# Sum of squares from a Gram matrix on TensorE, in a Fourier-layer tokenizer followed by a transformer layer

## The chip, the cores and the metric

The kernel runs on one core of one Trainium2 chip. The metric is the device time of one execution in microseconds. All data is float32. The engines are named as in the profile: PE is TensorE (PEld its weight loads), DVE is VectorE, ACT is ScalarE, POOL is GpSimd, SP is the engine whose queue issues most of the DMA.

## The reference, cut to what matters

64 images of 256x256 are lifted to 32 channels and pass four Fourier layers. Each layer adds a product in the frequency domain (12 frequencies along each edge) to a pointwise 32x32 product over the channels, normalises each channel by the mean and variance over all images and pixels, and applies a ReLU (not in the last). The resulting rows, with 77 text rows, go through one attention and one feed-forward block, which the change doesn't touch.

```python
for i in range(L):
    x1 = _fourier_layer(v, W1, W2)
    x2 = jnp.einsum('bcxy,cd->bdxy', v, w_w[i]) + w_b[i][None, :, None, None]
    v = x1 + x2
    mean = jnp.mean(v, axis=(0, 2, 3), keepdims=True)
    var = jnp.var(v, axis=(0, 2, 3), keepdims=True)
    v = (v - mean) * jax.lax.rsqrt(var + BN_EPS)
    v = v * bn_g[i][None, :, None, None] + bn_b[i][None, :, None, None]
    if i < L - 1:
        v = jax.nn.relu(v)
```

For the variance of layer i+1 the kernel needs, for each channel d, the sum over all pixels of the square of (v W)[d], where W is the pointwise matrix of layer i+1. The rest of the variance comes from the few frequencies.

## The kernel before

The kernel alternates two kinds of stage. `mix(i, ...)` multiplies the frequencies by the weights and works out the scale and shift of the normalisation. `layer(i, ...)` (three times, i = 0, 1, 2) then makes the image of the layer, applies the ReLU, stores it to memory, and takes the next layer's frequencies from it. After the last mix comes the transformer stage.

Inside `layer` the order of instructions is written out by hand: a loop over the images b, and in it over eight tiles t of an image, issues the steps below, and each engine runs its instructions in that order. One tile is 128 partitions (four row bands n of 32 channels) by 2048 pixels.

- `spread(b)` (L595 on PE, L599 on DVE): the inverse transform along x of image b, two PSUM tiles, each transposed by DVE into `y_`. It is issued at t=5 of the image before.
- `pre(b, t)`: the inverse transform along y (L614) and, in layers 1 and 2, the pointwise product of the layer's input `vin` (L625), accumulated in two PSUM tiles of two banks. ACT evicts the first with a ReLU (L632), DVE the second (L633), into the SBUF tile `vo`. SP stores `vo` (L634), and DVE transposes it in 32x32 blocks into `t32` (L637), one `t32` for two tiles; so `t32` holds pixels on partitions and channels along the free axis.
- `product(b, t)`, issued one tile behind `pre`: the next layer's pointwise product of `vo` (L649, 16 matmuls of 32x32 by 512) into two more PSUM tiles; ACT squares each and sums it along the row into a column of `acc` (L656).
- `along_y(b - 1)` at t=1: the forward transform along y of the four `t32` of the image before (L666, 128 matmuls), two PSUM tiles, transposed by DVE into `zt` (L676).
- `along_x(b - 1)` at t=3: the forward transform along x (L689), copied by ACT (L696) and stored (L697).

The loads of `vin` are issued on SP four tiles ahead. All PSUM tiles of a layer come from one ring `lp` of four tiles of two banks, the whole of the PSUM, used in turn: an instruction that writes a tile waits for the readers of the tile that had the place before.

After a layer, `squares(i, acc)` sums `acc` along the row, and a matmul with the table `CHAN` adds the partitions of the same channel, which gives `u2` to `mix`.

Of the kernel before, what the change touches and what calls it, by code (L numbers as in the profile page):

```python
# [9 lines left out]
F32 = mybir.dt.float32  # L10
# [24 lines left out]
def _tables():  # L35
# [47 lines left out]
    out["chan"] = p[:, None] % C == np.arange(C)[None, :]  # L83
# [46 lines left out]
def tile_fno_fusion_transformer(ctx: ExitStack, tc: tile.TileContext, a, cst_d, grid_d, out):  # L130
# [17 lines left out]
    tab = tables(const, "fyt", "chan", "cst")  # L148
# [3 lines left out]
    T4, ID, ONES, CHAN = tab("t4"), tab("ident"), tab("ones"), tab("chan")  # L152
# [336 lines left out]
    def squares(i, acc):  # L489

        u2 = const.tile([128, C], F32, name=f"u2_{i}")
        with tc.tile_pool(name="sq", bufs=1) as sp, tc.tile_pool(name="sqp", bufs=1, space=PSUM) as pp:
            r = sp.tile([128, 1], F32, name="r")
            nc.vector.reduce_sum(r, acc, axis=AX.X)
            rb = sp.tile([128, 128], F32, name="rb")
            nc.vector.tensor_copy(rb, r.to_broadcast([128, 128]))
            ps = pp.tile([128, C], F32, name="ps")
            nc.tensor.matmul(ps, lhsT=rb, rhs=CHAN, start=True, stop=True)
            nc.vector.tensor_copy(u2, ps)
        return u2  # L500

    def layer(i, st, src, dst, acc):
# [7 lines left out]
        with ExitStack() as cx:  # L510
# [9 lines left out]
            pp = pool("lp", 4, space=PSUM)  # L520
# [38 lines left out]
            am, y_, t32, vin, vo = {}, {}, {}, {}, {}  # L559
# [49 lines left out]
            def pre(b, t):  # L609
# [20 lines left out]
                o = vo[b, t] = op.tile([128, 8, S], F32, name="vo")  # L630
                of = o.rearrange("p (n r) y -> p n (r y)", r=2)
                nc.scalar.activation(of[:, 0:2], t2[0], AF.Relu)  # L632
                nc.vector.tensor_scalar(of[:, 2:4], t2[1], 0.0, None, ALU.max)  # L633
# [8 lines left out]
            def product(b, t):  # L642

                o = vo.pop((b, t))
                t2, ps = four()
                for k in range(4):
                    for n in range(4):
                        j = (n + k) % 4
                        nc.tensor.matmul(  # L649
                            ps[n][32 * j:32 * j + 32], lhsT=w4[i + 1][32 * n:32 * n + 32],  # L650
                            rhs=o[32 * n:32 * n + 32, 2 * j:2 * j + 2, :], start=True, stop=True,
                            skip_group_check=True, tile_position=(32 * n, 32 * j),
                        )
                for n in range(2):
                    at = 2 * (8 * b + t) + n
                    nc.scalar.activation(t2[n], t2[n], AF.Square, accum_out=acc[:, at:at + 1])  # L656
# [3 lines left out]
            def along_y(b):  # L660
# [11 lines left out]
                for j in range(4):  # L672
                    t32.pop((b, j))
                zt = zts[b] = zp.tile([128, 2, 32, C], F32, name="zt")
                for h in range(2):
                    nc.vector.transpose(  # L676
                        zt[:, h].rearrange("p k c -> p c k"),
                        t2[h].rearrange("p n (s c) -> p c (n s)", c=C),
                    )

            def along_x(b):
                zt = zts.pop(b)
                ps = pp.tile([128, 2, 512], F32, name="ring")
                for g in range(3):
                    n = 0
                    for h in range(2):
                        for r in range(2):
                            k0 = M * r + 4 * g
                            nc.tensor.matmul(  # L689
                                ps[:, 0, 96 * g:96 * g + 96],  # L690
# [5 lines left out]
                nc.scalar.copy(xo, ps[:, 0, 0:288].rearrange("p (g k) -> p g k", g=3)[:, :, 0:2 * KX])  # L696
# [10 lines left out]
            for b in range(B + 1):  # L707
                for t in range(8):
# [5 lines left out]
                    pb, pt = (b, t - 1) if t else (b - 1, 7)  # L714
                    if pb >= 0 and (b < B or t == 0):
                        product(pb, pt)
                    if b and t == 1:
                        along_y(b - 1)
                    if b and t == 3:
                        along_x(b - 1)  # L720
# [11 lines left out]
    acc = None  # L732
    for i in range(L):
        with tc.tile_pool(name="wn", bufs=2 if i else 1, reuse_waits="tile") as wnp, \
# [7 lines left out]
            else:  # L742
# [4 lines left out]
                u2 = squares(i, acc)  # L747
# [4 lines left out]
        if i < L - 1:  # L752
            acc = const.tile([128, 16 * B], F32, name="acc") if acc is None else acc
            with tc.manual_schedule():
                layer(i, st, vd[(i + 1) % 2], vd[i % 2], acc)
# [374 lines left out]
```

## Time and profile before

| what | us |
|---|---|
| median of three runs | 12480.16 |
| lowest and highest | 12466.59, 12493.44 |
| the profiled execution | 12478.37 |
| its span | 12476.6 |

| stretch (first `along_y` of the layer to the next stage), us | PE | DVE | ACT | PE clock | DMA share | GB/s |
|---|---|---|---|---|---|---|
| 293.8 to 3109.3, layer 0 | 2563.29 | 2177.00 | 1572.51 | 0.94 | 0.53 | 201 |
| 3305.9 to 6405.0, layer 1 | 2863.01 | 2217.49 | 1605.67 | 0.99 | 0.90 | 348 |
| 6603.4 to 9693.9, layer 2 | 2856.29 | 2216.19 | 1605.88 | 0.99 | 0.90 | 349 |
| 9693.9 to 12476.0, end of layer 2, last mix, transformer | 2575.19 | 1807.21 | 1013.60 | 0.97 | 0.58 | 220 |

How to read it: the second table gives busy time of each engine in each stretch. Matmuls are pipelined and the recorded ends overlap, so a busy PE isn't PE at its peak. The DMA share is the mean over the core's 16 DMA engines. In the profile's rows, "128*64 128x512" means a stationary operand of 128 rows and 64 columns and a moving one of 128 rows and 512 columns; an arrow after a stretch of idle time names what ended it, and "issue" means that the profile shows nothing that the engine waited for.

### The profile page before, as it was taken

The numbers are of one execution on the slowest core, as the hardware profiler recorded it, in microseconds if no ns is written. First come the engines' busy times: TensorE is split into PE (matmuls) and PEld (weight loads), VectorE is DVE, ScalarE is ACT, GpSimd is POOL, SyncE is SP. The second block draws the span as 40 slices with busy tenths as digits, with TensorE's granted clock in tenths as the row PEclk, the third lists the DMA queues.
The fourth block names the chain that finished last, engine by engine and source line by source line (L and its number), as shares of the span: only waits on it lengthen the run. The fifth ranks groups of instructions, "written<-read, shape, count | busy, mean of one in ns | idle before, by whom it ended". The sixth has DMA issues, their size and how long they took to land. (4 is left out here: it accounts for less than half of the span.)

```text
span 12476.6 us, 405217 instructions
## 1 busy us (share of the span) xinstructions
PE 11172.7 (90%) x182038; PEld 5874.2 (47%) x182038; DVE 8784.2 (70%) x10531; ACT 6065.1 (49%) x10217; POOL 1529.5 (12%) x2040
## 2 busy tenths in 40 slices
PE   4999999999699999999969999999999599999999
PEld 2444444444344444444434444444444366666666
DVE  4777777777677777777767776777777566666665
ACT  4555555555455555555545555555555333333333
POOL 1000000000100000000010000000000233333333
PEclk7999999999799999999989999999999799999999
DMA  6555555555899899889889898899899755555553
GB/s 187 199 202 202 201 202 202 200 201 203 286 350 350 346 351 353 344 345 349 341 277 358 345 354 347 341 351 352 345 352 352 255 218 229 232 227 221 221 231 151
DMA packets 588469, 3485.04 MB, mean 279 GB/s; under 512 B 96616, under 2 KB 146152, under 8 KB 189800
## 3 DMA queue, kind: packets, MB, share of 16 engines
q1 hardware_dynamic: 540288, 3405.18, 70.9%
q0 software_dynamic: 38144, 50.22, 1.8%
q8 instruction: 1423, 23.31, 0.7%
q10 hardware_dynamic: 8296, 3.72, 0.1%
q14 instruction: 318, 2.61, 0.1%
HBM read 1761.83 MB, written 1696.92 MB: 277 GB/s over the span
## 5 line engine op out<-in xcount | busy, mean ns | idle before, releaser
L656 ACT ACTIVATE ring<-ring 128x1024 f32<-128x1024 f32 x3072 | 3108.8, 1012 | 1185.5 <-PE ring L649 1148.6
L637 DVE STREAM_TRANSPOSE t<-vo 128x2048 f32<-128x2048 f32 x1536 | 3550.1, 2311 | 175.2 <-ACT vo L632 13.5
L649 PE MATMUL ring<-vo,w 32*32 32x512 f32 x49152 | 2851.0, 625 | 385.4 <-DVE zt L676 134.1
L632 ACT ACTIVATE vo<-ring 128x1024 f32<-128x1024 f32 x1536 | 1568.1, 1021 | 3045.8 <-PE ring L625 2386.1
L633 DVE TENSOR_SCALAR vo<-ring 128x1024 f32<-128x1024 f32 x1536 | 1858.6, 1210 | 615.0 <-PE ring L625 420.5
L666 PE MATMUL ring<-t,cst 32*32 32x512 f32 x49152 | 1867.6, 603 | 297.8 <-issue 296.6
L676 DVE STREAM_TRANSPOSE zt<-ring 128x1024 f32<-128x1024 f32 x384 | 712.3, 1926 | 1646.6 <-PE ring L666 1646.6
L649 PEld LDWEIGHTS ring<-vo,w 32*32 32x32 f32 x49152 | 765.5, 105 | 1886.4 <-ACT ring L656 473.7
L584 POOL TENSOR_TENSOR ams<-am,sk 48x512 f32<-48x512 f32 x384 | 486.7, 1268 | 8538.7 <-DMA am<-mix 8218.2
L666 PEld LDWEIGHTS ring<-t,cst 32*32 32x32 f32 x49152 | 976.3, 103 | 1145.6 <-issue 688.7
L625 PE MATMUL ring<-vin,ws 32*32 32x512 f32 x32768 | 1241.9, 607 | 21.2 <-issue 19.2
L689 PEld LDWEIGHTS ring<-cst,zt 128*128 128x128 f32 x4608 | 536.1, 194 | 179.4 <-ACT vo L632 159.5
L1079 POOL DMA_DIRECT2D out_dram<-o x1024 | 512.3, 509 | 660.1 <-DVE o L1074 628.8
L656 ACT ACTIVATION_READ_ACCUMULATOR ring<-ring 128x1 f32 x3072 | 584.2, 190 | 0.0
L689 PE MATMUL ring<-cst,zt 128*128 128x96 f32 x4608 | 568.3, 280 | 8.3 <-DVE zt L676 8.3
L878 PE MATMUL hp<-ch,win 128*32 128x512 f32 x4096 | 473.3, 602 | 8.6 <-DMA ch<-v 8.5
L595 PE MATMUL ring<-ams,cst 49*128 49x512 f32 (+1 forms) x1536 | 391.5, 620 | 99.4 <-POOL ams L584 88.7
L625 PEld LDWEIGHTS ring<-vin,ws 32*32 32x32 f32 x32768 | 253.8, 103 | 410.0 <-issue 382.8
L883 ACT ACTIVATE h<-hp,hbias 128x512 f32<-128x512 f32 x64 | 44.0, 687 | 597.5 <-PE hp L878 581.4
L412 PE MATMUL mps<-wm,xh 32*64 32x128 f32 (+1 forms) x4608 | 110.4, 354 | 242.2 <-DMA xh<-xh 110.8
L595 PEld LDWEIGHTS ring<-ams,cst 49*128 49x128 f32 (+1 forms) x1536 | 147.5, 188 | 349.8 <-issue 242.1
L1041 PE MATMUL pp<-zs,w 128*128 128x165 f32 x2048 | 302.4, 305 | 0.0
(932 smaller groups left out, 12039.4 us busy)
## 6 DMA issues: line engine op xcount, KB each, us to landing
v<-vo SPq DMA_DIRECT2D x1536, 1024.0 KB
vin<-v SPq DMA_DIRECT2D x1024, 1024.0 KB
ch<-v SPq DMA_DIRECT2D x512, 1024.0 KB
mix<-ob SPq DMA_DIRECT2D x192, 256.0 KB
am<-mix SPq DMA_DIRECT2D x384, 96.0 KB
xin<-in_x_dram SPq DMA_DIRECT2D x16, 1024.0 KB
mv<-in_x_dram SPq DMA_DIRECT2D x256, 64.0 KB
out_dram<-o POOLq DMA_DIRECT2D x1024, 16.0 KB, 3.0
```

Of the source, the lines that this page charges most:

```text
L584: nc.gpsimd.tensor_tensor(ams[b % 2][hv], a_[hv], sk[hv].rearrange("p c k -> p (c k)"), ALU.mult)
L595: nc.tensor.matmul(ps[:, n, :], lhsT=EX[hv, 128 * h:128 * h + 128], rhs=ams[b % 2][hv], start=True, stop=True, skip_group_check=True,)
L625: nc.tensor.matmul(ps[n][32 * j:32 * j + 32], lhsT=ws[32 * n:32 * n + 32], rhs=v[32 * n:32 * n + 32, 2 * j:2 * j + 2, :], start=False, sto ...
L632: nc.scalar.activation(of[:, 0:2], t2[0], AF.Relu)
L633: nc.vector.tensor_scalar(of[:, 2:4], t2[1], 0.0, None, ALU.max)
L637: nc.vector.transpose(t32[b, t // 2][:, :, 8 * (t % 2):8 * (t % 2) + 8, :].rearrange("p y s c -> p s y c"), o.rearrange("p s (y l) -> p s ...
L649: nc.tensor.matmul(ps[n][32 * j:32 * j + 32], lhsT=w4[i + 1][32 * n:32 * n + 32], rhs=o[32 * n:32 * n + 32, 2 * j:2 * j + 2, :], start=Tru ...
L656: nc.scalar.activation(t2[n], t2[n], AF.Square, accum_out=acc[:, at:at + 1])
L666: nc.tensor.matmul(ps[n][32 * j:32 * j + 32], lhsT=FYT[32 * n:32 * n + 32, k, :], rhs=t32[b, j][32 * n:32 * n + 32, k].rearrange("p s c -> ...
L676: nc.vector.transpose(zt[:, h].rearrange("p k c -> p c k"), t2[h].rearrange("p n (s c) -> p c (n s)", c=C),)
L689: nc.tensor.matmul(ps[:, 0, 96 * g:96 * g + 96], lhsT=zt[:, h, k0:k0 + 4, :].rearrange("p k c -> p (k c)"), rhs=FX[:, h, 48 * r:48 * r + 9 ...
L1079: nc.gpsimd.dma_start(out[b, 64 * n + 16 * g:64 * n + 16 * g + 16].rearrange("(p t) d -> p t d", t=2), o[32 * g + 8 * n:32 * g + 8 * n + 8 ...
```

## The change

The product of the next layer isn't formed any more. With G the 32x32 Gram matrix of the channels (G[c, c'] is the sum over all pixels of v[c] v[c']), the sum of squares of channel d is the sum over c and c' of W[c, d] G[c, c'] W[c', d].

- `product` and its squares on ACT go. `products(b, j, half)` takes a half of the transposed tile `t32[b, j]`: 32 matmuls, each with the same 128x64 slice as stationary and as moving operand (two pixels of 32 channels), accumulated over the whole image in one 128x64 PSUM tile. Even slices write partitions 0 to 63, odd ones 64 to 127. After the image, DVE adds the tile to `gram` in SBUF. The eight halves of an image are issued at t=3, 4, 5 and 6 (t32 0 and 1), and, an image later, two at t=0 and two at t=1 behind `along_y`.
- Both evictions of `pre` are now made by ACT.
- `along_y` hands its first PSUM tile to ACT, which copies it to `zs`; DVE transposes the second from PSUM and the first from `zs`.
- The ring `lp` has three tiles of two banks; `along_x` and the Gram matrix have one bank each.
- `squares` masks `gram` with a new table `DIAG` (32x32 blocks on the diagonal), multiplies it by W, then by W again element by element, and sums over the partitions with two matmuls.

```diff
@@ -486,20 +486,23 @@
-    def squares(i, acc):
+    def squares(i, gram):
...
-            r = sp.tile([128, 1], F32, name="r")
-            nc.vector.reduce_sum(r, acc, axis=AX.X)
-            rb = sp.tile([128, 128], F32, name="rb")
-            nc.vector.tensor_copy(rb, r.to_broadcast([128, 128]))
+            gm = sp.tile([128, 64], F32, name="gm")
+            nc.vector.tensor_mul(gm, gram, DIAG)
+            ps = pp.tile([128, C], F32, name="gw")
+            nc.tensor.matmul(ps[0:64], lhsT=gm, rhs=w4[i], start=True, stop=True)
+            wgw = sp.tile([64, C], F32, name="wgw")
+            nc.vector.tensor_mul(wgw, ps[0:64], w4[i][0:64])
             ps = pp.tile([128, C], F32, name="ps")
-            nc.tensor.matmul(ps, lhsT=rb, rhs=CHAN, start=True, stop=True)
+            nc.tensor.matmul(ps, lhsT=ONES[0:64], rhs=wgw, start=True, stop=True)
             nc.vector.tensor_copy(u2, ps)
...
-            pp = pool("lp", 4, space=PSUM)
+            pp = pool("lp", 3, space=PSUM)
+            px, pg = pool("lpx", 1, space=PSUM), pool("lpg", 1, space=PSUM)
+            nc.vector.memset(gram, 0.0)
...
-                o = vo[b, t] = op.tile([128, 8, S], F32, name="vo")
+                o = op.tile([128, 8, S], F32, name="vo")
                 of = o.rearrange("p (n r) y -> p n (r y)", r=2)
-                nc.scalar.activation(of[:, 0:2], t2[0], AF.Relu)
-                nc.vector.tensor_scalar(of[:, 2:4], t2[1], 0.0, None, ALU.max)
+                for n in range(2):
+                    nc.scalar.activation(of[:, 2 * n:2 * n + 2], t2[n], AF.Relu)
...
-            def product(b, t):
-
-                o = vo.pop((b, t))
-                t2, ps = four()
-                for k in range(4):
+            def products(b, j, half):
+
+                if (j, half) == (0, 0):
+                    gps[b] = pg.tile([128, 64], F32, name="gp")
+                q = t32[b, j]
+                for y in range(4 * half, 4 * half + 4):
+                    for m in range(8):
+                        d = 64 * (m % 2)
+                        v = q[:, y, 2 * m:2 * m + 2, :].rearrange("p s c -> p (s c)")
+                        nc.tensor.matmul(
+                            gps[b][d:d + 64], lhsT=v, rhs=v, start=(j, y) == (0, 0) and m < 2,
+                            stop=(j, y) == (3, 7) and m > 5, skip_group_check=True,
+                        )
+                if (j, half) == (3, 1):
+                    nc.vector.tensor_add(gram, gram, gps.pop(b))
                     for n in range(4):
-                        j = (n + k) % 4
-                        nc.tensor.matmul(
-                            ps[n][32 * j:32 * j + 32], lhsT=w4[i + 1][32 * n:32 * n + 32],
-                            rhs=o[32 * n:32 * n + 32, 2 * j:2 * j + 2, :], start=True, stop=True,
-                            skip_group_check=True, tile_position=(32 * n, 32 * j),
-                        )
-                for n in range(2):
-                    at = 2 * (8 * b + t) + n
-                    nc.scalar.activation(t2[n], t2[n], AF.Square, accum_out=acc[:, at:at + 1])
+                        t32.pop((b, n))
...
                 zt = zts[b] = zp.tile([128, 2, 32, C], F32, name="zt")
-                for h in range(2):
+                zs = zp.tile([128, 1024], F32, name="zs")
+                nc.scalar.copy(zs, t2[0].rearrange("p n k -> p (n k)"))
+                for h, z in ((1, t2[1].rearrange("p n k -> p (n k)")), (0, zs)):
...
-                ps = pp.tile([128, 2, 512], F32, name="ring")
+                ps = px.tile([128, 288], F32, name="xps")
...
-                    pb, pt = (b, t - 1) if t else (b - 1, 7)
-                    if pb >= 0 and (b < B or t == 0):
-                        product(pb, pt)
-                    if b and t == 1:
-                        along_y(b - 1)
-                    if b and t == 3:
-                        along_x(b - 1)
+                    if b:
+                        if t == 0:
+                            products(b - 1, 2, 0)
+                            products(b - 1, 2, 1)
+                        if t == 1:
+                            along_y(b - 1)
+                            products(b - 1, 3, 0)
+                            products(b - 1, 3, 1)
+                        if t == 3:
+                            along_x(b - 1)
+                    if b < B and t in (3, 4, 5, 6):
+                        products(b, (t - 3) // 2, (t - 3) % 2)
```

## The prediction

> **What bounds the kernel now.** First the page's busy shares and slices, to see which stages there are; then the groups, for the cost of each operation; then the order of time inside one image, because the shares average over stages.
>
> ```profile
> PE 11172.7 (90%) x182038; PEld 5874.2 (47%) x182038; DVE 8784.2 (70%) x10531; ACT 6065.1 (49%) x10217; POOL 1529.5 (12%) x2040
> ...
> PE   4999999999699999999969999999999599999999
> ...
> DMA  6555555555899899889889898899899755555553
> ```
>
> Three long stages of some 9 slices each are the three layer loops of 64 images; the rest (first transform, three mixes, the transformer) is not touched. In the order of time the first `along_y` (L666) of layer 0 starts at 293.8 and the last at 3109.3, 63 images later: 44.7 us an image. Layer 1: 3305.9 to 6405.0, 49.2; layer 2: 6603.4 to 9693.9, 49.1. PE reads as 9 tenths, but its bars overlap and hide waits.
>
> ```profile
> L656 ACT ACTIVATE ring<-ring 128x1024 f32<-128x1024 f32 x3072 | 3108.8, 1012 | 1185.5 <-PE ring L649 1148.6
> L637 DVE STREAM_TRANSPOSE t<-vo 128x2048 f32<-128x2048 f32 x1536 | 3550.1, 2311 | 175.2 <-ACT vo L632 13.5
> L649 PE MATMUL ring<-vo,w 32*32 32x512 f32 x49152 | 2851.0, 625 | 385.4 <-DVE zt L676 134.1
> L632 ACT ACTIVATE vo<-ring 128x1024 f32<-128x1024 f32 x1536 | 1568.1, 1021 | 3045.8 <-PE ring L625 2386.1
> L633 DVE TENSOR_SCALAR vo<-ring 128x1024 f32<-128x1024 f32 x1536 | 1858.6, 1210 | 615.0 <-PE ring L625 420.5
> ```
>
> The columns are total busy time, mean ns, idle time before. L649 shows x49152 = 192 images x 128 matmuls x 2: each float32 matmul is recorded as two passes. One tile step of layer 1 or 2 in order of time (start, length):
>
> ```profile
> 4512.53 0.99 PEld L614 LDWEIGHTS ring<-cst,y__46047 24*128 24x128 f32 x16 [0.91 <-ACT vo L632]
> 4512.53 1.40 PE L614 MATMUL ring<-cst,y__46047 24*128 24x256 f32 x16
> ...
> 4513.86 1.14 PE L625 MATMUL ring<-vin,ws 32*32 32x512 f32 x32
> ...
> 4514.74 1.49 PE L649 MATMUL ring<-vo,w 32*32 32x512 f32 x32
> 4514.74 0.58 PEld L649 LDWEIGHTS ring<-vo,w 32*32 32x32 f32 x31 [0.32 <-issue]
> 4515.15 1.02 ACT L632 ACTIVATE vo<-ring 128x1024 f32<-128x1024 f32 x1 [0.44 <-PE ring L625]
> 4515.21 1.22 DVE L633 TENSOR_SCALAR vo<-ring 128x1024 f32<-128x1024 f32 x1
> ```
>
> The step (3.7 us) is `pre` on PE, then both evictions side by side, then the next `pre`, which waits for its ring slot ("<-ACT vo L632"). The product matmuls L649 run in the shadow of the evictions: they cost PE about 1 us a step (two rounds of 0.43, and a tail) and hardly any time of the image. DVE (1.21 + 2.31 = 3.52 us a step) is nearly as full. Over `along_y` PE is alone: 8.73 us in layer 0 (2000.47 to the next L614 at 2009.20), about 11 in layers 1 and 2, where PE pauses for nothing the profile shows:
>
> ```profile
> 3505.13 6.46 PE L666 MATMUL ring<-t,cst 32*32 32x512 f32 x174
> 3512.84 3.28 PE L666 MATMUL ring<-t,cst 32*32 32x512 f32 x82 [1.25 <-issue]
> 3516.05 1.15 PE L614 MATMUL ring<-cst,y__34227 24*128 24x256 f32 x16
> ```
>
> The DMA table has an instruction queue of 1423 packets and 23.31 MB, 16 KB each. PE has 2 x 182038 matmuls and weight loads: 64 B each, so a packet is 256 of them. I take these pauses for late instruction fetches, since they are long only where DMA is 9 tenths busy. In this image (3505.13 to the next L666 at 3552.99, 47.9) they add to about 3.5 us, so without them layers 1 and 2 stand at 44.4, with a mean of 4.7 us of pauses; layer 0 has images of 43.74 (2000.47 to 2044.21) without any, so 1.0.
>
> **What the Trainium skill says.** "TensorE: Matmul & The Clock Gate", section LDWEIGHTS: a weight load takes its columns / 1.2 ns, whatever the rows. The trace agrees: `along_x` (L689) loads 128 columns 24 times in 2.75 us, (2.75 - 0.19) / 23 = 111 ns against 107. "TensorEngine Tiling (Array Packing)", Key Properties: tiles load and multiply independently, and a change of tiling mode drains the engine. It agrees for the first transform, whose 128x64 tiles are of the new shape: 8 passes of 512 columns took 1.94 us, in four rounds of two, so (1.94 - 0.64) / 3 = 0.43 us a round, 0.85 ns a column, with two at once. But the first page's Part 3 says that loads overlap running matmuls only if the row group differs; in L689 all rows are the same, and a pass of 96 columns (0.08 us) with a load of 111 ns comes every 111 ns: overlapped. I follow the trace.
>
> **The change part by part.**
>
> *Removed, each image:* 8 products on PE, 8 x 1.0 = 8.0 us; 16 squares with accumulator reads on ACT, 16 x (1.01 + 0.19); 8 DVE evictions of 1.21. *Added:* 8 evictions of 1.02 and the copy `zs` (1.0) on ACT. ACT then has 16 x 1.02 + 1.0 + 0.3 = 17.6 us an image; DVE 8 x 2.31 and four transposes of 1.9 = 26. Neither bounds; ACT and DVE gains are worth nothing by themselves.
>
> *Added on PE:* 256 matmuls of a 128x64 stationary and 64 moving columns, on two column tiles in turn: 512 passes, 256 rounds of two. A round is the longer of 64 columns streamed (64 x 0.85 = 54 ns) and 64 loaded (111 / 2 = 56): I take 58, as nothing this short is shown; bounds 54 (both hidden, nothing between) and 112 (load and stream in turn). 256 x 58 = 14.85 us. The six blocks of them (two are double) each pay some 0.25 us of first load and drain: 16.4 us an image. Bounds 13.8 and 30.
>
> *PE's other work:* `pre` from L614 to L625 1.07, L625 with its tail 1.03: 2.1 x 8 = 16.8 (layer 0 without L625: 1.22 x 8 = 9.8); `along_y` 8.7; `along_x` 2.95; `spread` 1.95. With the Gram 46.8 us, layer 0 39.8.
>
> *The ring of three.* A `pre` takes two tiles; the next begins in the third and then needs the first one's eviction. ACT ends that 2.3 us after L625 starts (4513.86 to 4516.17), PE is free after 1.03, and 0.1 of work fits: 1.2 us of wait where no Gram block stands between. That is at t=1 before `along_y`, t=2 and t=7. Elsewhere a block of 2.1 us covers it. At t=5 `spread`'s two tiles follow; `pre` of t=6 needs one back from DVE, which first does the 2.31 transpose behind two serial ACT evictions: 2.4 (ACT) + 2.31 + 1.84 = 6.6 us after the `pre`, PE arrives after 2.12 + 1.95: 2.4 us of wait. Sum 3 x 1.2 + 2.4 = 6.0; bounds 3 and 9. The second eviction moving behind the first makes `vo`, its store on SP, and the `vin` load queued behind that store about 0.9 us later; loads run four tiles ahead, so this is hidden. `zs` lies under 3.9 us of Gram, the two `zt` transposes end 4 us after `along_y`, long before `along_x` at t=3. With own banks for `along_x` and the Gram no further wait is added.
>
> *Pauses.* PE instructions an image go from 1856 to 2368 (layers 1, 2) and from 1344 to 1856 (layer 0). The stretch t=0 and t=1 now has 1216 of them in 22 us. I take 5.0 us of pauses in layers 1 and 2 (DMA has more time per byte, which works against the count), 1.0 in layer 0; bounds 3 and 10.
>
> *Sum.* Layers 1 and 2: 46.8 + 6.0 + 5.0 = 57.8, 8.7 more than 49.1, x128 = 1113. Layer 0: 39.8 + 6.0 + 1.0 = 46.8, 2.1 more than 44.7, x64 = 135. The last image's Gram of each layer stands alone, some 7 us x 3 = 20. `squares` swaps one short chain for another, and the constants grow by 32 columns, read once: nothing. 12476.6 + 1268 = 13745; the runs' median stands 3.6 above the span: 13,750.
>
> **Rivals.** *(A) Instruction supply bounds layers 1 and 2.* If 256 instructions cost 6.1 us there (174 + 82 passes with their loads, 512 instructions, took 10.9, so 5.5 with a stock at hand), 2368 need 56.4 us, and 4 to 5 us of ring waits beside it make 61; layer 0 at 49: 12477 + 1523 + 275 = 14,280. For it: the "issue" pauses; against it: they shrink where DMA has slack. *(B) Loads do not overlap in column tiles.* 112 ns a round, 13.8 us more an image: 12477 + 22.5 x 128 + 15.9 x 64 = 16,370. For it: the skill's sentence; against it L689 and the first transform. *(C) Faster: Gram blocks fill what PE waits for now.* Needed PE work is 46.8 and 39.8, under today's 49.1 and 44.7. If the blocks cover ring waits and fetches run ahead in them, so that these stay under 3.2 us an image together (my sum is 11 and 7), the kernel gains; at 1.5 us it is 12477 - 0.8 x 128 - 3.4 x 64 = 12,160. For it: today's waits end on evictions, which the third tile and the idle DVE relieve. Against it: three places have no block, and pauses grow with instructions.
>
> **How the numbers follow.** Forecast 0.58 (13,300 to 14,000); A 0.18; B 0.08; C 0.10; the remaining 0.06 lies between 12,450 and 13,300, some third of it within 0.2%. A measurement of this kernel can tell about 0.2% from no change. Faster 0.10, same 0.02, slower 0.88. The range from 12,900 to 14,500 takes in A and part of the rest, and leaves out B and C.
>
> **What would show it.** PE as the bound with ACT near 40% and DVE near half in the loops; `along_y` starts 57 to 59 us apart in layers 1 and 2, 46 to 48 in layer 0; a double Gram block (128 passes) of 3.7 to 4 us; PE waits on ACT at t=1, 2 and 7, and on DVE `y_` at t=6. A double block near 7.4 us is B; pauses within Gram blocks over 8 us an image are A; an image under 49 us makes the forecast wrong.

## The result, and the profile after

| | median us | lowest to highest | runs | profiled span |
|---|---|---|---|---|
| before | 12476.82 | 12466.59 to 12493.44 | 4 | 12476.6 |
| after | 13810.66 | 13802.2 to 13825.33 | 4 | 13823.6 |

The ratio is 1.1069 (95% interval 1.105 to 1.1088): the change makes the kernel 10.7% slower. The forecast was 13,750, its range 12,900 to 14,500.

From the page of the changed kernel: busy times, slices, and the queue of the instruction fetches.

```profile
PE 12182.1 (88%) x231196; PEld 8173.4 (59%) x231196; DVE 7036.9 (51%) x9190; ACT 4405.7 (32%) x5801; POOL 1529.6 (11%) x2040
...
PE   5999999996888888888868888888888869999999
...
PEclk7999999997999999999989999999999979999999
DMA  6555555557777777777777777777777775555554
...
q8 instruction: 1807, 29.61, 0.8%
```

DVE fell from 8784 to 7037 us and ACT from 6065 to 4406, and the end moved out by 1347. Layers 1 and 2 fill ten to eleven slices each, and DMA is down from 9 tenths to 7 in them, since the same bytes have more time. The clock row has 9 tenths in every slice that lies within a loop, but tenths hide a few us an image. PE has 2 x 49,158 more instructions, and the fetch queue has 384 more packets of 256 (2 x 49,158 / 256 = 384).

From one `along_y` start to the next (the first and the last of each layer, 63 images between), us an image:

| | layer 0 | layer 1 | layer 2 |
|---|---|---|---|
| before | 44.69 | 49.19 | 49.06 |
| after | 44.65 | 59.49 | 59.83 |
| forecast | 46.8 | 57.8 | 57.8 |

Layer 0 pays nothing. Layers 1 and 2 give 63 x (10.30 + 10.77) = 1327 of the 1347 us; the rest lies between the layers (14.0 us more between layers 0 and 1, 8.1 between 1 and 2).

From the groups of the changed kernel (busy, mean ns, idle before and what ended it):

```profile
L642 DVE STREAM_TRANSPOSE t<-vo 128x2048 f32<-128x2048 f32 x1536 | 3535.7, 2308 | 3988.2 <-ACT vo L638 3988.1
L638 ACT ACTIVATE vo<-ring 128x1024 f32<-128x1024 f32 x3072 | 2967.9, 1021 | 5268.6 <-PE ring L630 3998.1
...
L656 PE MATMUL gp<-t 128*64 128x64 f32 x98304 | 3286.2, 228 | 165.4 <-issue 164.6
L673 PE MATMUL ring<-t,cst 32*32 32x512 f32 x49152 | 2057.6, 616 | 336.8 <-issue 278.9
```

The product L649 and its squares are gone, both evictions are on ACT (L638), and the Gram is L656. DVE now waits for ACT, and ACT for PE: the slack of both has nothing to give. Part of an image of layer 1 in order of time, PE only:

```profile
4535.40 2.08 PE L656 MATMUL gp<-t 128*64 128x64 f32 x64
4537.41 1.99 PE L600 MATMUL ring<-ams,cst 49*128 49x512 f32 x8
4539.33 0.70 PE L619 MATMUL ring<-cst,y__52098 24*128 24x256 f32 x4
4541.66 2.08 PE L619 MATMUL ring<-cst,y__52098 24*128 24x256 f32 x12 [1.63 <-DVE y__52789 L604]
4543.67 2.01 PE L630 MATMUL ring<-vin,ws 32*32 32x512 f32 x32
4545.61 3.22 PE L656 MATMUL gp<-t 128*64 128x64 f32 x64
...
4552.20 1.13 PE L619 MATMUL ring<-cst,y__52789 24*128 24x256 f32 x12 [0.58 <-ACT vo L638]
4553.27 1.14 PE L630 MATMUL ring<-vin,ws 32*32 32x512 f32 x32
4554.34 3.95 PE L656 MATMUL gp<-t 128*64 128x64 f32 x128
...
4563.47 4.45 PE L673 MATMUL ring<-t,cst 32*32 32x512 f32 x128 [0.66 <-issue]
4569.69 3.38 PE L673 MATMUL ring<-t,cst 32*32 32x512 f32 x93 [1.76 <-issue]
```

Four things are to be seen. A double Gram block lasts 3.88 us from its start to the next matmul (4554.34 to 4558.22), so a round is (3.88 - 0.2) / 63 = 58 ns. The waits are at the places named: for DVE's transpose of `y_` at t=6 (1.63), for ACT's eviction in the pairs without a block (0.58 on the bar, some 1.2 in time). And something that was not foreseen: after the wait at t=6 the same matmuls take almost twice as long (L630 2.01 instead of 1.14, L656 3.22 instead of 2.08). That is PE at half clock: the record of the granted clock has it at half from 4541.32 to 4548.14. Last, the pauses: the one of 1.76 us in `along_y` comes just 128 passes after the one of 0.66, and 128 passes with their loads are 256 instructions, one packet of the queue.

### The profile page after: what moved, and what is told of

The parts are those of the page before. It is cut to its first block, busy times and chain, and to the rows that moved or that the text cites. A ratio compares the mean times of both kernels' runs of the same rounds, so it can differ in the third digit from the quotient of the medians.

```text
span 13823.6 us, 492594 instructions
## 1 busy us (share of the span) xinstructions
PE 12182.1 (88%) x231196; PEld 8173.4 (59%) x231196; DVE 7036.9 (51%) x9190; ACT 4405.7 (32%) x5801; POOL 1529.6 (11%) x2040
## 3 DMA queue, kind: packets, MB, share of 16 engines
q8 instruction: 1807, 29.61, 0.8%
## 5 line engine op out<-in xcount | busy, mean ns | idle before, releaser
L638 ACT ACTIVATE vo<-ring 128x1024 f32<-128x1024 f32 x3072 | 2967.9, 1021 | 5268.6 <-PE ring L630 3998.1
L656 PEld LDWEIGHTS gp<-t 128*64 128x64 f32 x98304 | 3104.4, 142 | 961.9 <-issue 901.9
L656 PE MATMUL gp<-t 128*64 128x64 f32 x98304 | 3286.2, 228 | 165.4 <-issue 164.6
L630 PE MATMUL ring<-vin,ws 32*32 32x512 f32 x32768 | 1306.3, 635 | 49.2 <-issue 48.8
L683 DVE STREAM_TRANSPOSE zt<-ring 128x1024 f32<-128x1024 f32 x192 | 380.0, 1979 | 1518.7 <-PE ring L673 1518.7
L681 ACT COPY zs<-ring 128x1024 f32<-128x1024 f32 x192 | 194.4, 1012 | 1937.6 <-PE ring L673 1937.6
L695 PEld LDWEIGHTS xps<-cst,zt 128*128 128x128 f32 x4608 | 528.9, 192 | 128.3 <-issue 127.7
L695 PE MATMUL xps<-cst,zt 128*128 128x96 f32 x4608 | 560.6, 278 | 1.3 <-issue 1.0
L630 PEld LDWEIGHTS ring<-vin,ws 32*32 32x32 f32 x32768 | 259.3, 105 | 452.6 <-issue 452.2
L683 DVE STREAM_TRANSPOSE zt<-zs 128x1024 f32<-128x1024 f32 x192 | 388.3, 2022 | 0.0
L1063 PE MATMUL pp<-g,w 128*128 128x165 f32 x2048 | 298.6, 303 | 0.0
L1063 PEld LDWEIGHTS pp<-g,w 128*128 128x128 f32 x2048 | 291.3, 189 | 0.0
```

What stands on the lines that cost most here:

```text
L630: nc.tensor.matmul(ps[n][32 * j:32 * j + 32], lhsT=ws[32 * n:32 * n + 32], rhs=v[32 * n:32 * n + 32, 2 * j:2 * j + 2, :], start=False, sto ...
L638: nc.scalar.activation(of[:, 2 * n:2 * n + 2], t2[n], AF.Relu)
L656: nc.tensor.matmul(gps[b][d:d + 64], lhsT=v, rhs=v, start=(j, y) == (0, 0) and m < 2, stop=(j, y) == (3, 7) and m > 5, skip_group_check=True,)
L683: nc.vector.transpose(zt[:, h].rearrange("p k c -> p c k"), z.rearrange("p (s c) -> p c s", c=C))
L695: nc.tensor.matmul(ps[:, 96 * g:96 * g + 96], lhsT=zt[:, h, k0:k0 + 4, :].rearrange("p k c -> p (k c)"), rhs=FX[:, h, 48 * r:48 * r + 96], ...
L1063: nc.tensor.matmul(ps[:, :KEPT], lhsT=w2[:, hb, 128 * dh:128 * dh + 128], rhs=g[:, hb, :], start=hb == 0, stop=hb == HID // 128 - 1,)
```

## The experiments

Each expectation names two theories (T1 and T2 below) and what both give. The diffs are against the changed kernel. "Median" is of timed runs with the interval of the ratio to the kernel before; where only one time is given the kernel was run once. "Half clock" is the time an image, from the record of the granted clock, in which PE ran at half speed; the record has no level but half and full here. A "pause" is idle time of PE that ends with "issue", that is, for which the profile shows no other engine.

| kernel | us | layer 0 / 1 / 2, us an image | half clock, us an image |
|---|---|---|---|
| before | 12476.8 | 44.69 / 49.19 / 49.06 | 5.3 / 1.3 / 0.8 |
| after | 13810.7 | 44.65 / 59.49 / 59.83 | 2.1 / 4.2 / 4.5 |
| half the instructions | 13335.9 | 44.41 / 55.65 / 56.08 | 3.3 / 4.2 / 4.8 |
| half the `vin` load | 13480.8 | 44.74 / 56.75 / 56.80 | 2.2 / 4.4 / 4.2 |
| four column tiles | 16698.7 | 55.40 / 76.93 / 76.74 | 19 / 32 / 32 |
| no Gram | 12419.1 | 36.74 / 52.51 / 52.16 | 13.4 / 22.0 / 20.7 |
| one eviction on DVE | 13656.4 | 44.79 / 58.46 / 58.54 | 2.8 / 3.0 / 3.2 |
| blocks spread | 13460.9 | 42.39 / 57.86 / 57.96 | 1.5 / 4.1 / 5.2 |
| `y_` first | 13386.0 | 41.80 / 57.70 / 57.35 | 0.0 / 2.4 / 2.4 |
| both orders | 13132.3 | 40.22 / 56.23 / 56.29 | 0.0 / 2.3 / 1.9 |
| bf16 | 12830.7 | 44.21 / 51.78 / 52.13 | 19.7 / 7.6 / 8.9 |
| bf16, one eviction on DVE | 12508.0 | 41.59 / 51.14 / 50.29 | 9.1 / 8.4 / 6.3 |
| the same, `y_` first | 11993.0 | 41.38 / 46.92 / 46.95 | 12.3 / 1.9 / 1.7 |
| the same, 128x128 | 11663.4 | 41.27 / 44.57 / 44.26 | 4.0 / 1.1 / 0.6 |

### What the added instructions cost

**Half the instructions, the same time in the array.** 128 matmuls of twice the moving columns take the place of 256.

```diff
-                    for m in range(8):
+                    for m in range(4):
                         d = 64 * (m % 2)
-                        v = q[:, y, 2 * m:2 * m + 2, :].rearrange("p s c -> p (s c)")
+                        v = q[:, y, 4 * m:4 * m + 4, :].rearrange("p s c -> p (s c)")
                         nc.tensor.matmul(
-                            gps[b][d:d + 64], lhsT=v, rhs=v, start=(j, y) == (0, 0) and m < 2,
+                            gps[b][d:d + 64], lhsT=v[:, 0:64], rhs=v, start=(j, y) == (0, 0) and m < 2,
```

> Half as many Gram matmuls, each with a moving operand of 128 columns for the same 64 stationary ones: the array streams as long, PE has 512 instructions an image less (the second half of the columns is not used, so half of the pixels is left out of the Gram matrix). Theory 1 (pauses are late instruction fetches, which go with the number of instructions): layers 1 and 2 fall from 59.6 to about 55 us an image, layer 0 by 1, total about 13150. Theory 2 (pauses come from elsewhere, the array time alone counts): only the fixed few ns of each matmul go, some 0.9 us an image, total about 13640.

Measured: 13335.85, nearer to T1 (13150) than to T2 (13640). Layers 1 and 2 fell by 3.8 us an image, layer 0 by 0.24. A single block lasts 1.90 us from its start to the next matmul, against 2.01, a double one 3.64 against 3.88, so at most 0.9 us an image of the 3.8 is array time (layer 0, with the same blocks, shows 0.24); half-clock time in layers 1 and 2 is the same. The rest is PE waiting for nothing the profile shows. The table of waits over 3350 to 6350 us (us in total, times, longest) in the changed kernel:

```profile
PE ring L673 <- issue: 107.7, 74, 2.6
PE gp L656 <- issue: 58.8, 59, 1.9
```

and in this one:

```profile
PE ring L673 <- issue: 63.3, 50, 2.3
PE gp L656 <- issue: 10.3, 13, 1.6
```

All such waits of PE in the window come to 195.0 us in the changed kernel (3.9 an image) and 73.6 here (1.4). So 512 instructions cost 2.9 to 3.6 us an image in layers 1 and 2 (3.8 less the array time), and next to nothing in layer 0. The bars make the pauses look shorter than they are, because the bars of the passes before a pause reach into it. Taken from the start of one pass to the start of the next, an estimate from the same traces, the pauses are 5.0 and 5.3 us an image in layers 1 and 2 of the changed kernel, 1.9 and 2.0 here, 3.7 in the kernel before, and 0.1 in layer 0 of the changed kernel.

**Half the load.** Only half of each `vin` tile is read, and the product uses that half twice.

```diff
-                nc.sync.dma_start(vin[b, t], src[b][:, t])
+                nc.sync.dma_start(vin[b, t][:, 0:4], src[b][:, t, 0:4])
...
-                                rhs=v[32 * n:32 * n + 32, 2 * j:2 * j + 2, :], start=False, stop=True,
+                                rhs=v[32 * n:32 * n + 32, 2 * (j % 2):2 * (j % 2) + 2, :], start=False, stop=True,
```

> Loads only half of every vin tile and uses that half twice (layers 1 and 2 then compute on half of their input): 4 MB an image less of 16.8, the instructions of PE unchanged. Theory 1 (a fetch is late because DMA is busy): pauses in layers 1 and 2 fall from 8.4 us towards the 1.0 of layer 0, an image takes about 53.5 us, total about 13050. Theory 2 (the number of instructions alone sets the pauses): no change within 1%, 13700 to 13830.

Measured: 13480.76, between T1 (13050) and T2 (no change). Layers 1 and 2 fell by 2.9 us with every instruction in place, and the pauses fell to 82.6 us in the same window (1.6 an image). So the pauses need both: many instructions and a loaded DMA.

What ends them can be read from the packets of the instruction queue, which the trace keeps with their times. In the same window of the changed kernel, 98% of the 160 pauses end 1.15 to 1.65 us after the end of a 16 KiB packet of that queue (median 1.41); of PE's 194 waits for other engines only 9% do. In layer 1 of the kernel before, of half the instructions, of four column tiles and of both orders (below) it is 98% or more of the pauses, against 13% or less of the other waits. So the pauses are instruction fetches that land late. The transfer itself isn't slower: a packet takes 0.96 us (median) in layer 0, where 7 pauses go with 430 packets, and 0.97 in layer 1, where 160 go with 467. What holds a packet up before its transfer no run shows directly; that half the load removes over half of the pauses points to the data ahead of it.

**More instructions, less time in the array.** The Gram of single pixels, 32 columns, on four column tiles: 512 matmuls an image. `squares` uses 32 partitions instead of 64.

```diff
-                    for m in range(8):
-                        d = 64 * (m % 2)
-                        v = q[:, y, 2 * m:2 * m + 2, :].rearrange("p s c -> p (s c)")
+                    for m in range(16):
+                        d = 32 * (m % 4)
+                        v = q[:, y, m, :]
```

> The Gram with 32-column operands on four column tiles: 512 matmuls an image, which need half the array time (256 rounds of about 32 ns, 8.2 us against 14.9), but 1024 PE instructions an image more (3392 in layers 1 and 2). Theory 1 (late fetches set layers 1 and 2): 3392 instructions at 6 us for 256 take 75 to 80 us an image there, layer 0 within 4 us of before, total about 16000. Theory 2 (array time alone): 6.7 us an image less, total about 12500.

Measured: 16698.72, worse by 2888 us; T1 had 16,000. Its table of waits in the same window (here the end of layer 0, the mix and the first half of layer 1):

```profile
PEld gp L654 <- issue: 756.9, 427, 7.8
PE gp L654 <- issue: 555.5, 226, 7.7
```

PE now stands in the middle of Gram blocks, up to 7.7 us at a time. 3392 instructions an image in 76.8 us are 5.8 us per 256; layer 0 has 2880 in 55.4 us, 4.9 per 256. At that count the supply is the bound, in layer 0 as well, which T1 had put within 4 us of before and which took 10.8 us more. PE is at half clock for 32 us an image in layers 1 and 2; 398 of the 436 half-clock stretches there have a pause as the longest wait within 4 us of their start.

**No Gram.** All Gram matmuls but the first and the last pair of an image are left out.

```diff
                     for m in range(8):
+                        if ((j, y) != (0, 0) or m > 1) and ((j, y) != (3, 7) or m < 6):
+                            continue
```

> Leaves out all Gram matmuls but the first and the last pair of each image (the variance of the next layer is then not the reference's); ring of three and ACT evictions stay. Theory 1 (the Gram's streaming is what the image pays): eight blocks of 15.9 us go, some five evictions lose their cover (+1.2 us each), pauses in layers 1 and 2 fall from 8.4 us to about 3: along_y starts some 35 us apart in layer 0 and 45 in layers 1 and 2, total about 11300. Theory 2 (the ring of three and the serial evictions on ACT cost the time): an image still over 47 us in layers 1 and 2, total over 12300.

Measured: 12419.1. Layer 0 stands at 36.7 us an image, near the 35 of T1. Layers 1 and 2, with the same 15.8 us of work taken out, fell by only 7.0 and 7.7 us, to 52.5 and 52.2: over 47, and the total over 12,300, as T2 has it. The order of time in layer 1 shows what takes the place of the Gram:

```profile
5020.74 2.08 PE L619 MATMUL ring<-cst,y__40055 24*128 24x256 f32 x12 [3.27 <-DVE y__40494 L604]
5022.75 2.01 PE L630 MATMUL ring<-vin,ws 32*32 32x512 f32 x32
5024.69 3.38 PE L619 MATMUL ring<-cst,y__40055 24*128 24x256 f32 x16
...
5038.49 2.01 PE L630 MATMUL ring<-vin,ws 32*32 32x512 f32 x32
5040.20 8.36 PE L675 MATMUL ring<-t,cst 32*32 32x512 f32 x196
```

Without the blocks as cover, the wait for DVE's `y_` at t=6 grows to 3.27 us. The clock is at half from 5018.34 to 5042.23, through the `pre`s that follow: L630 is still 2.01 us long 18 us later, and full speed is back only inside `along_y`. The bars show no idle time in between, but each `pre` holds a wait that they hide: from L619 to L630 it takes 3.30 us (5024.69 to 5027.99), where the kernel with four column tiles, at the same clock, takes 2.02. So this kernel doesn't measure the Gram by itself: ring waits, half clock and pauses fill what it leaves, and how much each takes isn't separated. Its variance, and so its data, is another too; no run shows whether that matters for the time.

### What the waits cost

**One eviction back on DVE.**

```diff
-                for n in range(2):
-                    nc.scalar.activation(of[:, 2 * n:2 * n + 2], t2[n], AF.Relu)
+                nc.scalar.activation(of[:, 0:2], t2[0], AF.Relu)
+                nc.vector.tensor_scalar(of[:, 2:4], t2[1], 0.0, None, ALU.max)
```

> The second eviction of pre goes back to DVE; all else as changed. Theory 1 (PE waits for the first eviction, which stays on ACT): only the wait of pre at t=6 on the transposes of spread gets shorter, 0.5 to 0.9 us an image, total about 13680 (13630 to 13720). Theory 2 (two serial evictions on ACT hold the ring): over 2 us an image, total under 13400.

Measured: 13656.44, ratio 1.0947 (1.0928 to 1.0965), as T1 has it. Two serial evictions instead of two side by side cost 1.0 to 1.3 us an image in layers 1 and 2 and nothing in layer 0.

**Blocks spread.** One Gram block behind each tile instead of two doubles around `along_y`.

```diff
-                        if t == 0:
-                            products(b - 1, 2, 0)
-                            products(b - 1, 2, 1)
+                        if t < 3:
+                            products(b - 1, (t + 5) // 2, (t + 5) % 2)
                         if t == 1:
                             along_y(b - 1)
-                            products(b - 1, 3, 0)
-                            products(b - 1, 3, 1)
...
-                    if b < B and t in (3, 4, 5, 6):
+                    if b < B and t > 2:
                         products(b, (t - 3) // 2, (t - 3) % 2)
```

> The eight Gram blocks stand one behind each tile (t=3 to 7, then t=0, 1, 2 of the next image; at t=1 ahead of along_y); same work and same instructions. Theory 1 (three places without a block wait for an eviction, 1.05 to 1.3 us each): 3.3 us an image less in every layer, pauses a little less as the bursts are broken up, total about 13150. Theory 2 (instruction supply sets layers 1 and 2): layer 0 gains 3.3 us, layers 1 and 2 stay within 1 us, total about 13550.

Measured: 13460.87, ratio 1.0794 (1.0776 to 1.0812), between the two and nearer to T2 (13550) than to T1 (13150). Layer 0 gained 2.3 us an image, what the two uncovered pairs were waiting; layers 1 and 2 gained 1.6 and 1.9.

**`y_` first.** `spread` goes directly behind `pre`'s matmuls at t=5, so that its two transposes on DVE are ahead of the 2.31 us one of `vo`.

```diff
                 nc.sync.dma_start(dst[b][:, t], o)
+                if t == 5 and b + 1 < B:
+                    spread(b + 1)
                 if t % 2 == 0:
...
-                        if t == 5:
-                            spread(b + 1)
```

> As changed, but at t=5 spread stands directly behind the matmuls of pre, and DVE transposes its two tiles before it transposes vo; the Gram block follows. Theory 1 (PE's wait for y_ at t=6 sends its clock to half speed for some 4 us of each image of layers 1 and 2): the wait of 1.5 to 2.3 us and most of the 4.2 us at low clock go, about 3.5 us an image less in layers 1 and 2 and 2 in layer 0, total about 13220. Theory 2 (late instruction fetches take the place of the wait): 1.5 us or less in layers 1 and 2, total 13450 or more.

Measured: 13385.97, ratio 1.0731 (1.0714 to 1.0747), between T1 (13220) and T2 (13450). Layer 0 gained 2.85 us, more than the wait at t=6 itself (2.3): half-clock time there went from 2.1 us to none. Layers 1 and 2 gained 1.8 and 2.5; half-clock time went from 4.3 to 2.4. It couldn't go to none: in the changed kernel only 67 of the 122 half-clock stretches of layers 1 and 2 start within 4 us of the wait for `y_`, and 54 start beside a pause; here 72 of the 74 that are left start beside a pause.

**Both orders.**

> Both orders together, still float32: one Gram block behind each tile (as e5) and spread with its transposes directly behind pre's matmuls at t=5 (as e11), so that no wait on the ring should be left. Changed kernel 13,811; e5 alone took 44.65 to 42.39 us an image in layer 0 and 59.6 to 57.9 in layers 1 and 2, e11 alone to 41.80 and 57.5. T1 (the waits are independent and add up): layer 0 at 39.6, which is the sum of PE's own work (39.8), layers 1 and 2 at 55.7; 13,811 - 5.0 x 64 - 3.9 x 128 = 12,990. T2 (what the waits leave is taken by late instructions, because PE runs through its stock sooner): layer 0 at 41, layers 1 and 2 at 57; 13,811 - 3.6 x 64 - 2.6 x 128 = 13,250. Under both the float32 Gram stays slower than the kernel before in layers 1 and 2 (49.1), because PE's own work with its loads is 46.8 and pauses of 9 or more are left.

Measured: 13132.28, ratio 1.0538 (1.0519 to 1.0558), midway between T1 and T2. In order of time, in layer 1:

```profile
4543.83 1.16 PE L630 MATMUL ring<-vin,ws 32*32 32x512 f32 x32
4544.92 1.62 PE L658 MATMUL gp<-t 128*64 128x64 f32 x48
4547.13 0.69 PE L658 MATMUL gp<-t 128*64 128x64 f32 x16 [0.59 <-issue]
4547.74 1.15 PE L619 MATMUL ring<-cst,y__56209 24*128 24x256 f32 x16
...
4561.65 4.46 PE L675 MATMUL ring<-t,cst 32*32 32x512 f32 x128 [0.23 <-issue]
4568.96 3.40 PE L675 MATMUL ring<-t,cst 32*32 32x512 f32 x96 [2.85 <-issue]
```

What is left are pauses: PE's waits for other engines come to 24.1 us over 3350 to 6350 us, 0.5 an image, where the changed kernel has 144.3. Layer 0 came to 40.2 us, near PE's own work. Layers 1 and 2 stay at 56.3, 7 us above the kernel before. The pauses in the same window sum to 238.5 us, 4.5 an image, against 3.9 in the changed kernel: with the waits gone the pauses grew somewhat, though half-clock time halved.

### A form that beats both

**bf16.** ACT, which has slack, copies each half of `t32` to bf16 one tile ahead of its use, and the Gram is taken from the copies (the sum of squares, and so the variance, comes from rounded values; all else stays float32). Blocks spread.

```diff
+            def lower(b, j, half):
+
+                q = low[b, j, half] = hp.tile([128, 4, 16, C], BF16, name="t16")
+                nc.scalar.copy(
+                    q.rearrange("p y s c -> p (y s c)"),
+                    t32[b, j][:, 4 * half:4 * half + 4].rearrange("p y s c -> p (y s c)"),
+                )
...
-                q = t32[b, j]
-                for y in range(4 * half, 4 * half + 4):
+                q = low.pop((b, j, half))
+                for y in range(4):
```

> ACT copies each half of t32 to bf16 one tile ahead (eight copies of about 1.8 us an image), and the Gram matmuls take these: one pass instead of two (512 PE instructions an image less, a quarter of the array time, about 4 us); blocks spread as above. Theory 1 (array time, ring waits and pauses add up): layer 0 about 37 us, layers 1 and 2 about 46.5 us an image, total about 11700, faster than both kernels. Theory 2 (supply of instructions, 1856 an image as in the kernel before): layers 1 and 2 at 49 or more, total about 12000.

Measured: 12830.73, ratio 1.029 (1.0275 to 1.0306). Both theories missed the total by over 800 us. One pass instead of two takes 256 passes and as many loads from the image, and layers 1 and 2 fell by 6 us against the spread blocks; but layer 0 rose from 42.4 to 44.2. The table of waits over 350 to 2800 us, layer 0:

```profile
PE gp L668 <- ACT t L654: 263.3, 300, 1.6
```

PE waits some five times an image, 0.9 us each, for ACT's copy (L654), which stands behind two evictions. And it runs at half clock for 19.7 of 44 us; 109 of the 152 half-clock stretches start beside such a wait, the others beside the one for `y_`.

**One eviction on DVE**, as above, to shorten that chain.

> As the bf16 kernel, with the second eviction of pre back on DVE. Theory 1: ACT is then shorter by 8 us and its copies come earlier, so PE waits less: 0.5 to 1.5 us an image less than with both evictions on ACT, total about 11500. Theory 2 (DVE with 36 us an image becomes the bound in layer 0): layer 0 longer by 1 us or more, total the same or above.

Measured: 12507.97, ratio 1.0036 (1.0023 to 1.0048): right in direction, 1000 us above the expectation. PE is still at half clock for 6 to 9 us an image.

**`y_` first**, as above, on top.

> The bf16 Gram with the second eviction on DVE (12508), with spread and its transposes ahead as in the other run. Theory 1 (waits at t=6 of 2.6 us and the low clock behind them, 8.4 us an image in layers 1 and 2): layer 0 about 38.5 us, layers 1 and 2 about 47, total about 11850, below the kernel before. Theory 2 (PE with so little to stream is at low clock whatever it waits for): 12200 or more.

Measured: 11992.98, ratio 0.9618 (0.9602 to 0.9634). Layers 1 and 2 fell by 3.3 to 4.2 us an image, to the 47 of T1, half-clock time from 6 to 8 us to below 2. Layer 0 stayed at 41.4, where T1 had 38.5, with half-clock time up from 9 to 12.

**128x128 operands**, on top: four pixels instead of two in each operand, half the Gram matmuls; DVE adds the four 32x32 blocks of the diagonal.

```diff
-                    for m in range(8):
-                        d = 64 * (m % 2)
-                        v = q[:, y, 2 * m:2 * m + 2, :].rearrange("p s c -> p (s c)")
+                    for m in range(4):
+                        v = q[:, y, 4 * m:4 * m + 4, :].rearrange("p s c -> p (s c)")
                         nc.tensor.matmul(
-                            gps[b][d:d + 64], lhsT=v, rhs=v, start=(j, y) == (0, 0) and m < 2,
+                            gps[b], lhsT=v, rhs=v, start=(j, half, y, m) == (0, 0, 0, 0),
```

> As the last, with 128x128 bf16 Gram matmuls of four pixels: 128 matmuls of about 57 ns an image (7.3 us) in place of 256 on two tiles (about 4 us), 256 PE instructions an image less. Theory 1 (array time, waits and pauses add up): 3 us more array time against about 1 us less of pauses, total 100 to 400 above the two-tile version. Theory 2 (low clock and late fetches decide): the denser PE keeps its clock and fetches less, total below the two-tile version.

Measured: 11663.42, ratio 0.9351 (0.9337 to 0.9365), as T2 has it and the best here. Its page and a piece of layer 1:

```profile
PE 10317.2 (89%) x157468; PEld 6546.8 (56%) x157468; DVE 8846.5 (76%) x11299; ACT 5770.1 (50%) x5801; POOL 1535.5 (13%) x2040
...
PEclk6999999999799999999979999999998999999999
DMA  6555555555899999999989999999998655555553
```

```profile
4546.70 1.07 PE L667 MATMUL gp<-t 128*128 128x128 bf16 x16
4547.69 1.43 PE L619 MATMUL ring<-cst,y__49870 24*128 24x256 f32 x16
4549.06 1.14 PE L630 MATMUL ring<-vin,ws 32*32 32x512 f32 x32
4550.41 1.07 PE L667 MATMUL gp<-t 128*128 128x128 bf16 x16 [0.21 <-ACT t L654]
```

DMA is back at 9 tenths in layers 1 and 2 and the clock is full there: the kernel moves the same bytes in less time than before, at a DMA share of 0.97, so little is left to gain there. A block takes 0.99 us, half of the float32 one, with 32 instructions instead of 128. The idea of the change (no second product, no squares) pays once PE's side of it is small: 1600 instructions an image in layers 1 and 2, against 1856 before and 2368 after. Of the last step's 2.4 to 2.7 us an image in layers 1 and 2, the pauses give most: on the bars they fell from 3.3 and 3.4 to 1.1 and 1.0. In layer 0 half-clock time fell from 12.3 to 4.0 and the layer's time not at all (41.4, 41.3); DVE is busy for 85% of it there, so PE seems no longer to set the time there, though no run shows that by itself.

## Why the prediction was right

The table has us an image. "Measured" takes each step, from its start to the next one's, at the shortest tenth of the images, with the waits taken off; `along_y` of layers 1 and 2 pauses in every image and stands at about its length in layer 0. The line of pauses is what the mean has above that sum. The working is good to some 0.2 us.

| term | forecast, layer 0 | measured | forecast, layers 1, 2 | measured |
|---|---|---|---|---|
| PE's own work | 39.8 | 37.8 | 46.8 | 46.4 |
| of it the Gram | 16.4 | 15.8 | 16.4 | 15.8 |
| ring waits | 6.0 | 5.8 | 6.0 | 5.0 |
| pauses | 1.0 | 1.0 | 5.0 | 8.3 |
| image | 46.8 | 44.65 | 57.8 | 59.66 |

The forecast missed by 79 us of span, and that is partly luck, because two errors meet in it: layer 0 was put 2.15 us an image too high and layers 1 and 2 some 1.9 too low.

- **What goes is worth little: right.** ACT and DVE lost over 3,400 us of work together, and the time rose. In layers 1 and 2 the Gram's 15.8 us run in the open, where the product (8 us an image by the prediction) had run under the evictions. Layer 0 took in the same 15.8 us and didn't grow, so there what went, with the waits around it, had cost the image about as much; no run takes it away alone. The sign "ACT near 40%" came in layer 0 alone (37%; 28% in layers 1 and 2), and the prediction's own 17.6 of 57.8 us is 30%.
- **The Gram on PE: right.** 58 ns a round taken, 58 measured; a double block 3.88 us, inside 3.7 to 4. Load and stream overlap although both column tiles use all rows, so the measurement stands against the sentence of the skill that rival B rests on, and its 7.4 us a block is out. The drain at a change of tiling mode no run here shows by itself.
- **PE's other work: right in layers 1 and 2; in layer 0 the mis-sized term.** The prediction took 1.22 us for a `pre` without L630. With a Gram block or another `pre` behind it, it lasts 1.08, 1.1 us an image less; the Gram's blocks are 0.6 shorter too.
- **Ring waits: right in place, and nearly in size.** `along_y` 1.1, the pairs at t=2 and t=7 1.2 to 1.3 each, t=6 2.3 in layer 0 and 1.3 in layers 1 and 2, where L630, 1.07 us long, stands between. The two experiments on order took them away at these places: layer 0 fell by 4.4 us of the 5.8 with both.
- **Pauses in layers 1 and 2: the mis-sized term, 8.3 for 5.0.** The prediction set the wider time per byte against the added instructions and took almost no growth from the 4.7 us before. The runs show growth: without the added instructions 2.9 to 3.6 of it is gone. The pauses proper, taken from start to start, are 5.0 to 5.3 of the 8.3 us; by the same count the kernel before has 3.7, where the prediction took 4.7. So a good part of what is missing isn't pauses at all but PE at half clock, which the prediction did not have: 4.3 us an image at half speed lose at most 2.2, behind the wait at t=6 and behind pauses. The last us isn't resolved. The pauses are late instruction fetches; the number of instructions and the load on DMA can't be told apart in them, since either experiment took off about 3 us and the two overlap.
- **Nothing from the second eviction's delay: wrong by a little.** It was priced in the ring waits and nowhere else; taking it back gave 1.0 to 1.3 us an image in layers 1 and 2, and nothing in layer 0.
- **Rival A** (supply as the bound, 61 and 49 us an image) had the right cause for the pauses, and layers 1 and 2, at 59.7, lie nearer to it than to the forecast. But layer 0 is 4 us below its figure, and the pauses inside Gram blocks are 58.8 us over 50 images, 1.2 an image against the 8 it asked for. The kernel with four column tiles is what A looks like.
- **Rival C** needed waits and pauses under 3.2 us an image together. With both orders, layer 0 of the float32 Gram reaches 40.2 and gains; layers 1 and 2 don't, since the pauses stay.

The Trainium skill, page "Runtime: NRT & Kernel Launch", section "Instruction fetch mechanics", says that each engine's instructions come in blocks of 16 KiB, 256 instructions, by a DMA queue of its own, and that crossing a block is mostly hidden. The packets agree (29.61 MB / 1807 = 16.4 KB). "Mostly hidden" holds in layer 0 of the changed kernel (7 pauses for 430 packets), and not in layer 1 (160 for 467), where the DMA engines are busy for 0.76 of the time instead of 0.54.

## What to carry to other kernels

Price an algebraic saving by the engine that bounds: here two engines were relieved and the third got 15.8 us an image of short matmuls in place of 8 that were partly hidden. Count the instructions of such matmuls as well as their array time, because a float32 product of 64 columns costs four instructions (two passes, two loads) for 58 ns of the array. When PE must wait, order the engine that frees its PSUM so that the wait is short: here a wait of 1.6 us was followed by 6.5 us of work at half speed.

## What the runs showed of the hardware

- **PE's pauses end a fixed time after an instruction packet lands.** In layers 1 and 2 of the changed kernel, 98% or more of them end 1.15 to 1.65 us after the end of a 16 KiB packet of the instruction queue, against 9% or less of PE's waits for other engines.
- **A stall of PE can cost more than its length.** With `y_` first, layer 0 gained 2.85 us for a wait of 2.3, and layers 1 and 2 gained 1.8 and 2.5 for one of 1.3. Every stretch at half clock lasts a whole multiple of 3.41 us in the loops of the changed kernel: 6.82 with the wait of 1.63 us shown above. With no Gram, the one shown is 23.89 us, with a wait of 3.27 at its start and PE in and out of waits until `along_y`. The Trainium skill, "TensorE: Matmul & The Clock Gate", Part 1, has half clock after an idle window of about 3.4 us and full clock after a busy one as long; here the first came after less, and the second came only in a dense stretch.
- **Instructions have a rate.** With the Gram on four column tiles, where PE stands in the middle of blocks, it got 256 instructions per 5.8 us in layers 1 and 2 (DMA share 0.61) and per 4.9 us in layer 0 (0.44).
- **bf16 operands of 128 columns load faster.** Load and stream of 128 x 128 in bf16 take 62 ns together (0.99 us / 16), so a load takes no more than that, where the prediction read 111 ns for a float32 load of 128 columns. The same page, section "Weight-path perf modes", says that loads of 128 columns that are not float32 are read some two times faster; this agrees.
